# Moving steps of a hand-written order: the second layer's attention of a two-layer transformer on one core

## The chip, the core and the metric

The kernel runs on one core of a Trainium2 chip. The metric is the device time of one execution in microseconds (us). Before the change it is 630.8 us, the median of three runs (625.72 to 632.23). The core has five engines that each work through their own instructions in order: PE (TensorE, matrix products), DVE (VectorE), ACT (ScalarE), POOL (GpSimd) and SP (SyncE, here only a queue of DMA issues). An instruction that waits holds up everything behind it on its engine.

## What is computed

Two layers over x, 8 batches of 256 tokens with 128 channels. Each layer norms and modulates x by a per-batch condition, adds a gated causal attention with 16 heads, norms and modulates again, and adds a gated mixture of experts. Cut to the second layer, which the change is about (`ca`, `sa`, `ga`, `cb`, `sb`, `gb` are rows per batch):

```
h = layernorm(x) * (1 + ca) + sa
q, k, v = h @ w_q, h @ w_k, h @ w_v                  # 16 heads of 64
w = softmax(causal(q k^T) / 8)
x = x + ga * (concat(w v) @ w_o)
h = layernorm(x) * (1 + cb) + sb
r = sigmoid(h @ gate_w + gate_b); top 2 of 16 experts, values divided by their sum
x = x + gb * (h + shared_mlp(h) + sum of 2 expert mlps, weighted)
```

The second layer's attention needs x with the first layer's experts already added; the sparse experts of layer 2 need the choices of batches 0 to 5 (batches 6 and 7 go through all experts densely).

## The kernel before

In the profile layer 0 (its attention, then its experts) ends at about 263 us, layer 1's attention runs from 265.5 to 531 us, and layer 1's experts from 531 us to the end. Everything from layer 0's attention on is in an order written out by hand: the order of the Python calls is the order of each engine's instructions. The framework adds the waits and the buffers; a tile tag with n buffers makes the (n+1)th user wait for the first one's last reader. Tag `p` in PSUM has two buffers and serves every projection, norm transpose, choice and output product.

The attention works in 32 units, four per batch; unit n is batch n // 4, and covers four heads. For a unit `project_qk1` (L1548) makes q and k (eight 128x256 matmul records on PE at L1554, copied out by ACT at L1558), `scores1` (L1575) makes scores of four heads (PE L1585), exponentials (ACT L1588) and the causal mask (POOL `affine_select`, L812). Two units make a pair p = 0 to 15. `values1` (L1596) multiplies a pair's weights by v (PE L1613), copies the unnormalised output `ou` out (DVE L1617), and sums the weights (PE L1623). After the second pair of a batch `reciprocals1` (L1628) takes 1 / sum on DVE (L1630) and spreads it through DRAM to a tile `rb` by DMA (L1635, L1638). `normalise1` (L1645) multiplies `ou` by `rb`, four 128x512 DVE operations per batch (L1647). `finish1` (L1661) makes the output product `y` (PE L1667, 32 records) and adds it to x (DVE L1673, L1674).

The loop over pairs, with tables of steps (`first`, `mid`, `last`, `late`) that are run at fixed places of each pair; `heads` holds steps to run after one head's mask inside `scores1`:

```
for p in range(N // 2):
    scores(2 * p + 1)
    run(first, p)
    project(2 * p + 3)
    if p + 1 < N // 2: project_v1(p + 1, 0)
    run(mid, p)
    project(2 * p + 4)
    if p + 1 < N // 2: project_v1(p + 1, 1)
    run(last, p)
    scores(2 * p + 2)
    values1(p)
    if p % 2 and p + 1 < N // 2: reciprocals1(p // 2)
    run(late, p)
```

The steps in these tables, before the change:

- The first layer's experts' outputs: `gather(b, j)` (two indirect DMAs each, issued by POOL at L1047), `combine` (six DVE operations, L1365 to L1369). Batches 2 and 3 are gathered inside units 0 and 1, combined late in pair 0.
- The first norm: `measure` (DVE statistics L746, L748, then two small POOL operations L751, L752 for the reciprocal deviation), `normalise` (DVE L762), `modulate` (PE transposes L771, then h on DVE L774). Batch 1's measure and normalise stand ahead of pair 0, its modulate at `mid` 0, ahead of unit 4's projection.
- `sel`, a constant made by POOL (L2025, L2026) after unit 0's scores and needed only after the attention.
- `normalise1(b)` at `late` of pair 2b + 2, `finish1(b)` at `first` of pair 2b + 3.
- The second norm and the choice (`norm1`, `route1`, steps called `go`): batches 0 and 1 together from pair 5, 2 and 3 from pair 9, 4 from pair 11, 5 from pair 13. `route1` makes logits (PE L1716), the top two (17 short DVE operations, L1722 to L903), counts of earlier tokens (POOL `seen` L907, PE `rk` L910 and L911), slots (DVE `at` L913 to `idx` L919), then scatters of the tokens to DRAM by indirect DMA (POOL L924), one after a head's mask. `tokens` and `add` are POOL operations (L1690 to L1696).
- The tables of the experts' tiles (`tables_steps`, PE `cnt` L954, then 14 DVE operations L957 to L995) at `last` 14; they give the indices `widx` and `rowi` by which SP fetches experts' weights (L1771, `fetch_weights1`) and rows (L1749, `fetch_rows1`).

After pair 15 the experts begin with the transpose of the first fetched rows (PE L1786 `xT`).

Of the kernel before, what the change touches and what calls it, by code (L numbers as in the profile page):

```python
# [13 lines left out]
ALU = mybir.AluOpType  # L14
# [10 lines left out]
D0, D1 = 8, 64  # L25
# [532 lines left out]
def fast_path(ctx: ExitStack, tc: tile.TileContext, i: dict, out: bass.AP, bad: bass.AP):  # L558
# [300 lines left out]
    class Sorted:  # L859
# [184 lines left out]
        def gather(self, yg, j):  # L1044

            for k in range(2):
                nc.gpsimd.indirect_dma_start(  # L1047
                    out=yg[:, k, :], out_offset=None, in_=self.ys[:, :],
                    in_offset=bass.IndirectOffsetOnAxis(ap=self.yidx[:, j, k : k + 1], axis=0),
                )  # L1050
# [594 lines left out]
    def normalise1(b, u):  # L1645
        aT = st1["ou", b]
        nc.vector.tensor_tensor(aT[:, :, u, :], aT[:, :, u, :], st1["rb", b][:, :, u, :], ALU.mult)  # L1647
# [97 lines left out]
    def fetch_rows1(m):  # L1745

        xg = sq["x", m] = lp.tile([P, 4, P], F32, tag="xg", bufs=4, name=f"xg1_{m}")
        if m < E1 // 4:
            nc.sync.dma_start(  # L1749
                out=xg, in_=z1.xs.rearrange("(e r) c -> r e c", r=z1.cap)[0:P, bass.ts(m, 4), :]  # L1750
            )
        else:
            for t in range(4):
                z1.load_rows(xg[:, t, :], 4 * m + t - E1, starts.pop(0))

    def find_rows1(m):

        starts.extend(z1.row_starts(4 * m - E1, 4))
# [189 lines left out]
    def to(where, p, *steps):  # L1948
        where.setdefault(p, []).extend(steps)

    def at_scores(n, head, step):

        heads.setdefault(n, {}).setdefault(head, []).append(step)
# [5 lines left out]
    def combine_later(b):  # L1959
        return lambda: combine(b)  # L1960
# [6 lines left out]
    project_qk1(0, 1)  # L1967
    measure, normalise, modulate = layernorm_parts(0, md[1], SA, CA, "1a1", ps_ln, tiles=range(2, TT))
    for j in range(2):
        at_scores(0, 1 + 2 * j, lambda j=j: gather(2, j))  # L1970
        at_scores(1, 1 + 2 * j, lambda j=j: gather(3, j))
    to(first, -1, combine_later(1), measure, normalise)
    to(mid, 0, modulate)
    for w, n in ((1, 0), (2, 3), (3, 7)):
        measure, normalise, modulate = first_norm(w)
        if w == 1:
            to(late, 0, combine_later(2), combine_later(3), measure)
            to(late, 1, normalise)
        else:
            for k in range(4):  # L1980
                at_scores(8 * w - 13 + k, 3, lambda w=w, k=k: gather(2 * w + k // 2, k % 2))
            to(late, n, combine_later(2 * w))
            to(first, n + 1, combine_later(2 * w + 1))
            to(last, n + 1, measure)
            to(late, n + 1, normalise)
        to(mid, 4 * w - 2 if w == 1 else n + 2, modulate)
    for b in range(B - 1):
        to(late, 2 * b + 2, *[lambda b=b, u=u: normalise1(b, u) for u in range(4)])
        to(first, 2 * b + 3, lambda b=b: finish1(b))
    for bs in ((0, 2), (2, 2), (4, 1), (5, 1)):  # L1990
        p = 2 * sum(bs) + 1
        measure, normalise, modulate, tokens, add = norm1(bs)
        go = one(route1(bs))
        if bs[0] < 5:
            to(last, p, measure)
            to(late, p, normalise)
            to(first if bs[0] == 4 else mid, p + 1, modulate, tokens)
            to(last, p + 1, go)
            to(late, p + 1, go, go, go, go)
            to(mid, p + 2, go)  # L2000
            for k in range(4 * bs[1] - 1):
                at_scores(2 * p + 6 + k // 2, 1 + 2 * (k % 2), go)
            to(late, p + 3, add)
        else:
            to(first, p, measure)
            to(last, p, normalise, modulate, tokens)
            to(first, p + 1, go, go, go, go, go)
            to(last, p + 1, go)
            for k in range(3):
                at_scores(2 * p + 4, 1 + k, go)  # L2010
    tables = one(z1.tables_steps(ps_ln, True))
    to(last, 14, tables, lambda: fetch_weights1(4), lambda: fetch_weights1(5))
    to(first, 15, *[lambda m=m: fetch_rows1(m) for m in range(4)], *[lambda m=m: find_rows1(m) for m in range(4, NQ)],
       lambda: fetch_weights1(6))

    def scores(n):
# [3 lines left out]
    def project(n):  # L2020
        if n < N:
            project_qk1(*divmod(n, 4))

    scores(0)
    nc.gpsimd.memset(sel, 0.0)  # L2025
    nc.gpsimd.affine_select(  # L2026
        out=sel, in_=sel, compare_op=ALU.not_equal, fill=1.0, base=0,
        pattern=[[-8, 4], [-32, 2], [-64, 2], [0, D1]], channel_multiplier=1,
    )
    run(first, -1)  # L2030
    project(2)
    for p in range(N // 2):
# [3 lines that stand above are left out]
        if p + 1 < N // 2:  # L2036
            project_v1(p + 1, 0)
        run(mid, p)
        project(2 * p + 4)
        if p + 1 < N // 2:  # L2040
            project_v1(p + 1, 1)
        run(last, p)
        scores(2 * p + 2)
        values1(p)
        if p % 2 and p + 1 < N // 2:
            reciprocals1(p // 2)
        run(late, p)
# [209 lines left out]
```

## Time and profile before

| what | us |
|---|---|
| median of three runs (lowest, highest) | 630.8 (625.72, 632.23) |
| the profiled execution, its own time | 630.67 |
| its span, first to last instruction | 628.6 |
| PE busy, DVE, POOL, ACT | 541.1, 326.6, 309.9, 265.6 |
| mean granted TensorE clock | 0.94 |
| PE busy in 265 to 290, 290 to 525, 525 to 575, 575 to 630 | 18.66, 223.42, 43.85, 32.19 |

The profile is of one execution. Busy time is the time in which an engine has an instruction in work; matmuls overlap, so PE can be busy for the whole of a stretch. A view by windows gives the busy time of each engine in stretches; here the stretches are the pairs, each from the start of `scores(2p+1)` to that of the next. A view of waits gives who waited for whom. The timeline gives instructions in order, in columns start, duration, engine, line, operation, output and inputs, count, and in brackets the idle time ahead of it and what ended it. The chain of waits goes back from the last instruction through what released each step.

### The profile page before, as it was taken

Reading aid. Unit: us, or ns where it says so; the run is one execution under the profiler, and the core shown is the slowest. Engines: PE = TensorE matmul, PEld = TensorE weight load, DVE = VectorE, ACT = ScalarE, POOL = GpSimd, SP = SyncE. Lnnn points to the kernel's source line nnn. Section 1 sums busy time; section 2 is a strip of 40 time slices with the busy share of each in tenths; the row PEclk is TensorE's granted clock in tenths of the full one; section 3 lists DMA queues with packets and bytes.
Section 4 is the critical chain, followed back from the end, with each engine's and each line's share of the span. In section 5 each row is a group of like instructions: output and inputs, shape, how many; then the busy total and the mean of one; then the engine's idle time right before and its main releaser. Section 6 shows DMA issues by size and latency. Waiting matters only on the chain.

```text
span 628.6 us, 11934 instructions
## 1 busy us (share of the span) xinstructions
PE 541.1 (86%) x4391; PEld 389.3 (62%) x4391; DVE 326.6 (52%) x1031; ACT 265.6 (42%) x489; POOL 309.9 (49%) x472
## 2 busy tenths in 40 slices
PE   3799879878799999687999999989998898888961
PEld 3344435445699998455777767667776666665451
DVE  3347896856732222311543645473544676654683
ACT  1475675546065555162544353433534432330330
POOL 7356686866314441365551444572356664203760
PEclk9998988879999999896999999999999999888996
DMA  8999980120329996040030303030203036562431
GB/s 279 346 407 404 388 315 13 61 90 29 113 82 328 327 321 214 22 163 22 19 86 2 72 15 86 15 85 5 69 9 90 10 90 177 164 183 73 113 90 56
DMA packets 52909, 85.38 MB, mean 136 GB/s; under 512 B 6428, under 2 KB 32156, under 8 KB 51692
## 3 DMA queue, kind: packets, MB, share of 16 engines
q1 hardware_dynamic: 44444, 59.77, 29.9%
q0 software_dynamic: 8400, 24.78, 12.7%
q8 instruction: 36, 0.59, 0.4%
q14 instruction: 29, 0.24, 0.1%
HBM read 53.46 MB, written 31.07 MB: 134 GB/s over the span
## 4 chain that ended last, share of the span: by engine, by line
PE 58%; DVE 18%; POOL 8%; DMA 6%; issue 4%; ACT 4%; SPq 0%; DVEq 0%; POOLq 0%; ACTq 0%
PE o L1613 7%; PE hp L1338 6%; PE sc L1585 5%; PE yt L1346 5%; POOL yg L1047 5%; PE qp L1554 4%; PE kp L1554 4%; PE vp L1567 4%; PE sc L1137 3%; DVE ou L1647 3%; PE y L1667 3%; PE sum L1623 3%; PE o L1162 2%; PE qk L1101 2%; PE gu L1797 1%
## 5 line engine op out<-in xcount | busy, mean ns | idle before, releaser
L812 POOL TENSOR_SCALAR_AFFINE_SELECT pt<-pt 128x256 f32<-128x256 f32 (+1 forms) x176 | 91.1, 542 | 90.4 <-ACT pt L1588 59.9
L1588 ACT ACTIVATE pt<-sc 128x768 f32<-128x768 f32 x64 | 48.5, 808 | 71.1 <-PE sc L1585 70.9
L1047 POOL DMA_INDIRECT yg<-ys,yidx x56 | 54.3, 969 | 29.7 <-issue 14.6
L1617 DVE COPY ou<-o 128x512 f32<-128x512 f32 x32 | 22.0, 691 | 68.9 <-PE o L1613 68.9
L1141 ACT ACTIVATE pt<-sc 128x1024 f32<-128x1024 f32 x48 | 46.5, 1022 | 17.6 <-PE sc L1137 14.4
L1039 POOL DMA_INDIRECT wt<-in_wpk_dram,widx x31 | 29.1, 939 | 48.8 <-PE xT L1329 47.3
L1340 ACT ACTIVATE hst<-hp,wt 128x128 f32<-128x128 f32 x136 | 38.8, 367 | 30.0 <-ACT hst L1340 17.9
L1585 PEld LDWEIGHTS sc<-q,k 64*128 64x128 f32 x512 | 41.8, 188 | 15.5 <-issue 12.4
L1585 PE MATMUL sc<-q,k 64*128 64x256 f32 (+1 forms) x512 | 50.8, 338 | 0.0
L1558 ACT COPY q<-qp 128x512 f32<-128x512 f32 x32 | 18.7, 585 | 63.1 <-PE qp L1554 62.6
L1613 PE MATMUL o<-pt,v 128*64 128x256 f32 (+1 forms) x512 | 45.1, 329 | 0.0
L1137 PE MATMUL sc<-qm,k 32*128 32x512 f32 x192 | 38.3, 731 | 3.9 <-ACT pt L1141 3.0
L1350 DVE COPY ysb<-yt 128x128 f32<-128x128 f32 x39 | 11.4, 292 | 58.0 <-PE yt L1346 58.0
L1554 PE MATMUL qp<-h,wq 128*128 128x256 f32 x128 | 36.8, 412 | 4.7 <-DVE h L774 1.5
L1613 PEld LDWEIGHTS o<-pt,v 128*64 128x64 f32 x512 | 32.0, 137 | 11.2
L1667 PE MATMUL y<-wo,ou 128*128 128x128 f32 x256 | 34.2, 291 | 5.1 <-DVE ou L1647 5.0
L1338 PE MATMUL hp<-xTs,wt 128*128 128x128 f32 x272 | 36.9, 279 | 1.6 <-DMA wt<-in_wpk_dram,widx 0.9
L924 POOL DMA_INDIRECT xs<-ht0b,idx x32 | 31.6, 988 | 13.5 <-issue 4.7
L1554 PE MATMUL kp<-h,wk 128*128 128x256 f32 x128 | 35.6, 403 | 0.7 <-DVE t L1673 0.5
L1667 PEld LDWEIGHTS y<-wo,ou 128*128 128x128 f32 x256 | 31.5, 200 | 7.3 <-DVE ou L1647 6.2
L1346 PE MATMUL yt<-wt,hst 128*128 128x128 f32 x272 | 35.8, 275 | 0.0
L1567 PE MATMUL vp<-wv,h 128*128 128x512 f32 x64 | 35.6, 643 | 0.0
(292 smaller groups left out, 1095.2 us busy)
## 6 DMA issues: line engine op xcount, KB each, us to landing
xs<-zero SPq DMA_DIRECT2D x1, 12288.0 KB, 57.5
xs<-zero SPq DMA_DIRECT2D x1, 8192.0 KB, 26.4
rb<-rd SPq DMA_DIRECT2D x14, 512.0 KB, 5.8
mdb<-mrd SPq DMA_DIRECT2D x2, 2048.0 KB, 7.3
xg<-xs SPq DMA_DIRECT2D x63, 64.0 KB, 4.1
wt<-in_wpk_dram SPq DMA_DIRECT2D x24, 128.0 KB, 2.3
wst<-in_wpk_dram SPq DMA_DIRECT2D x5, 514.0 KB, 12.7
ys<-ysb SPq DMA_DIRECT2D x10, 256.0 KB, 2.7
```

The costliest lines, as they stand in the source:

```text
L812: nc.gpsimd.affine_select(out=pt, in_=pt, compare_op=ALU.is_ge, fill=0.0, base=0, pattern=[[0, pt.shape[1]], [1, P]], channel_multiplier=-1,)
L1047: nc.gpsimd.indirect_dma_start(out=yg[:, k, :], out_offset=None, in_=self.ys[:, :], in_offset=bass.IndirectOffsetOnAxis(ap=self.yidx[:, j, ...
L1137: nc.tensor.matmul(out=sc[:, n, :].rearrange("p (a q) -> p a q", q=rhs.shape[2]), lhsT=k[r, cols], rhs=rhs, start=True, stop=True,)
L1141: nc.scalar.activation(pt[:, bass.ts(half, 2), :], sc, AF.Exp)
L1338: nc.tensor.matmul(out=hp[:, c, :], lhsT=wt[:, bass.ts(c, P)], rhs=xT, start=True, stop=True)
L1346: nc.tensor.matmul(out=y, lhsT=hs[:, c, :], rhs=wt[:, bass.ds(WF + c * P, P)], start=(c == 0), stop=(c == FC - 1))
L1554: nc.tensor.matmul(out=ps_[:, n, :], lhsT=w1[f"w{what}1"][:, bass.ts(2 * u + n, P)], rhs=hb, start=True, stop=True)
L1567: nc.tensor.matmul(out=vp, lhsT=hb[:, bass.ts(j, P)], rhs=w1["wv1"][:, bass.ts(half, 512)], start=True, stop=True)
L1585: nc.tensor.matmul(out=sc[:, n, cols], lhsT=k[r, m, bass.ts(kb, P)], rhs=q[r, m, qs], start=True, stop=True)
L1588: nc.scalar.activation(pt, sc[:, :, 0:384], AF.Exp, scale=1.0 / math.sqrt(D1))
L1613: nc.tensor.matmul(out=os_[u][bass.ts(n, D1), m, qs], lhsT=v[:, kb, bass.ts(4 * k + 2 * m + n, D1)], rhs=pts[u][m][:, n, cols], start=(kb ...
L1667: nc.tensor.matmul(out=y[:, j, :], lhsT=aT[:, c % 2, c // 2, bass.ts(j, P)], rhs=w1["wo1"][:, c, :], start=(c == 0), stop=(c == NC1 - 1),)
```

## The change

Only the places of steps in the tables change; every engine executes as many instructions as before, in another order.

- The gathers of batches 2 and 3 move one unit later, to units 1 and 2. Batch 1's normalise moves to `mid` 0, its modulate to `first` 1, and unit 4's projection behind it. `combine` of batch 3 and the measure of batches 2 and 3 move into pair 1. `sel` is made at `mid` 3.
- `normalise1(b)` moves from `late` 2b + 2 to `mid` 2b + 3 (for b = 5 to `first` 13), `finish1(b)` from `first` to `last` of the same pair (for b = 5 to `mid` 13).
- Batch 4's modulate moves from `first` 12 to `mid` 12. Batch 5's measure, modulate and choice move later: measure to `mid` 13, modulate to `first` 14, directly ahead of its logits.
- The tables move from `last` 14 to `first` 15, the fetches of rows from `first` 15 to `mid` 15, after batch 6's normalise1.

```diff
@@ -1967,26 +1967,24 @@
     project_qk1(0, 1)
     measure, normalise, modulate = layernorm_parts(0, md[1], SA, CA, "1a1", ps_ln, tiles=range(2, TT))
     for j in range(2):
-        at_scores(0, 1 + 2 * j, lambda j=j: gather(2, j))
-        at_scores(1, 1 + 2 * j, lambda j=j: gather(3, j))
-    to(first, -1, combine_later(1), measure, normalise)
-    to(mid, 0, modulate)
+        at_scores(1, 1 + 2 * j, lambda j=j: gather(2, j))
+        at_scores(2, 1 + 2 * j, lambda j=j: gather(3, j))
+    to(first, -1, combine_later(1), measure)
+    to(mid, 0, normalise)
+    to(first, 1, modulate, lambda: project(4))
     for w, n in ((1, 0), (2, 3), (3, 7)):
         measure, normalise, modulate = first_norm(w)
-        if w == 1:
-            to(late, 0, combine_later(2), combine_later(3), measure)
-            to(late, 1, normalise)
-        else:
+        if w > 1:
             for k in range(4):
                 at_scores(8 * w - 13 + k, 3, lambda w=w, k=k: gather(2 * w + k // 2, k % 2))
-            to(late, n, combine_later(2 * w))
-            to(first, n + 1, combine_later(2 * w + 1))
-            to(last, n + 1, measure)
-            to(late, n + 1, normalise)
-        to(mid, 4 * w - 2 if w == 1 else n + 2, modulate)
+        to(late, n, combine_later(2 * w))
+        to(first, n + 1, combine_later(2 * w + 1))
+        to(last, n + 1, measure)
+        to(late, n + 1, normalise)
+        to(mid, n + 2, modulate)
     for b in range(B - 1):
-        to(late, 2 * b + 2, *[lambda b=b, u=u: normalise1(b, u) for u in range(4)])
-        to(first, 2 * b + 3, lambda b=b: finish1(b))
+        to(first if b == 5 else mid, 2 * b + 3, *[lambda b=b, u=u: normalise1(b, u) for u in range(4)])
+        to(mid if b == 5 else last, 2 * b + 3, lambda b=b: finish1(b))
     for bs in ((0, 2), (2, 2), (4, 1), (5, 1)):
         p = 2 * sum(bs) + 1
         measure, normalise, modulate, tokens, add = norm1(bs)
@@ -1994,7 +1992,7 @@
         if bs[0] < 5:
             to(last, p, measure)
             to(late, p, normalise)
-            to(first if bs[0] == 4 else mid, p + 1, modulate, tokens)
+            to(mid, p + 1, modulate, tokens)
             to(last, p + 1, go)
             to(late, p + 1, go, go, go, go)
             to(mid, p + 2, go)
@@ -2002,15 +2000,15 @@
                 at_scores(2 * p + 6 + k // 2, 1 + 2 * (k % 2), go)
             to(late, p + 3, add)
         else:
-            to(first, p, measure)
-            to(last, p, normalise, modulate, tokens)
-            to(first, p + 1, go, go, go, go, go)
+            to(mid, p, measure)
+            to(last, p, normalise)
+            to(first, p + 1, modulate, tokens, go, go, go, go, go)
             to(last, p + 1, go)
             for k in range(3):
                 at_scores(2 * p + 4, 1 + k, go)
     tables = one(z1.tables_steps(ps_ln, True))
-    to(last, 14, tables, lambda: fetch_weights1(4), lambda: fetch_weights1(5))
-    to(first, 15, *[lambda m=m: fetch_rows1(m) for m in range(4)], *[lambda m=m: find_rows1(m) for m in range(4, NQ)],
+    to(first, 15, tables, lambda: fetch_weights1(4), lambda: fetch_weights1(5))
+    to(mid, 15, *[lambda m=m: fetch_rows1(m) for m in range(4)], *[lambda m=m: find_rows1(m) for m in range(4, NQ)],
        lambda: fetch_weights1(6))
 
     def scores(n):
@@ -2021,12 +2019,15 @@
         if n < N:
             project_qk1(*divmod(n, 4))
 
+    def make_sel():
+        nc.gpsimd.memset(sel, 0.0)
+        nc.gpsimd.affine_select(
+            out=sel, in_=sel, compare_op=ALU.not_equal, fill=1.0, base=0,
+            pattern=[[-8, 4], [-32, 2], [-64, 2], [0, D1]], channel_multiplier=1,
+        )
+
+    to(mid, 3, make_sel)
     scores(0)
-    nc.gpsimd.memset(sel, 0.0)
-    nc.gpsimd.affine_select(
-        out=sel, in_=sel, compare_op=ALU.not_equal, fill=1.0, base=0,
-        pattern=[[-8, 4], [-32, 2], [-64, 2], [0, D1]], channel_multiplier=1,
-    )
     run(first, -1)
     project(2)
     for p in range(N // 2):
@@ -2036,7 +2037,8 @@
         if p + 1 < N // 2:
             project_v1(p + 1, 0)
         run(mid, p)
-        project(2 * p + 4)
+        if p:
+            project(2 * p + 4)
         if p + 1 < N // 2:
             project_v1(p + 1, 1)
         run(last, p)
```

## The prediction, made before the changed kernel ran

> **What bounds the kernel now.** I read the page first (which engines the chain of waits runs through), then the windows with one row per pair of layer 1's attention, then PE's waits in that stage, then the timeline where a pair is long.
>
> ```profile
> PE 58%; DVE 18%; POOL 8%; DMA 6%; issue 4%; ACT 4%; SPq 0%; DVEq 0%; POOLq 0%; ACTq 0%
> ```
> ```profile
> core 0: us, PE busy (x) PEld busy (x) DVE busy (x) ACT busy (x) POOL busy (x), PEclk, DMA share, GB/s
> 276.42:298.87 22.45, 16.64 (x120) 11.02 (x119) 3.49 (x10) 7.50 (x13) 14.72 (x23) 0.77 0.09 24
> 342.34:355.12 12.78, 12.78 (x118) 8.87 (x118) 10.06 (x29) 6.54 (x10) 4.70 (x10) 1.00 0.37 85
> 386.94:404.31 17.37, 16.94 (x156) 12.81 (x152) 8.57 (x28) 6.54 (x10) 7.16 (x16) 1.00 0.04 12
> 417.03:439.03 22.00, 19.56 (x158) 14.86 (x154) 10.08 (x20) 6.54 (x10) 10.31 (x15) 0.92 0.03 9
> 470.84:486.16 15.32, 13.60 (x126) 9.53 (x122) 6.03 (x11) 6.77 (x11) 8.99 (x15) 1.00 0.37 88
> 486.16:505.46 19.30, 17.54 (x156) 13.17 (x153) 12.07 (x35) 6.64 (x10) 13.06 (x21) 1.00 0.05 15
> 505.46:519.05 13.59, 12.14 (x119) 8.18 (x115) 11.38 (x37) 5.49 (x9) 7.64 (x14) 1.00 0.44 99
> 519.05:531.08 12.03, 10.12 (x117) 8.06 (x113) 7.88 (x13) 1.51 (x2) 6.89 (x11) 1.00 0.66 188
> ```
> These are pairs 0, 4, 7, 9, 12, 13, 14 and 15. Pair 4 has nothing added and PE is busy for all of its 12.78 us: PE is the bound, and only PE's waits can be won or lost. Pair 0 loses most, then pair 9.
>
> ```profile
> PE nt1a L771 <- DVE xn1a L762: 5.1, 1, 5.1
> PE y L1667 <- DVE ou L1647: 5.0, 5, 1.1
> PE nt1b L771 <- DVE xn1b L762: 1.7, 1, 1.7
> PE rk L910 <- DVE m L903: 1.2, 1, 1.2
> ```
> The 5.1 is in pair 0. Its cause stands on POOL: two gathers, `sel`, and only then the deviation that batch 1's normalise needs:
>
> ```profile
> 282.18 0.97 POOL L2025 MEMSET sel<- 128x1024 f32 x1
> 283.22 1.20 POOL L2026 TENSOR_SCALAR_AFFINE_SELECT sel<-sel 128x1024 f32<-128x1024 f32 x1
> ...
> 285.99 0.75 PE L771 MATMUL nt1a<-ident,xn1a 128*128 128x128 f32 x2 [5.08 <-DVE xn1a L762]
> ...
> 287.47 2.05 PE L1554 MATMUL qp<-h,wq 128*128 128x256 f32 x4 [0.73 <-DVE h L774]
> ```
> The reader sees the wait, and behind it a projection at 2.05 that takes 1.06 warm: the granted clock fell.
>
> **Part by part.** I walk PE through each changed pair, T being the start of its `scores(2p+1)`. Sizes from rows: scores 1.51, q and k of a unit 1.9, v 0.95, values 2.75, sums 1.44, y 3.78.
>
> *Pairs 0 and 1.* POOL now does the deviation right behind unit 0's masks, so normalise is done near 279. Pair 0 loses unit 4's q and k and has no wait: after v(1,0) at 280.9 come v 0.95, scores 1.51, values and sums 4.19, so pair 1 begins at 287.6, not 298.87. Unit 0 and 1's masks are ready: the last is behind two gather issues (1.26 each) at 282.7, values begin at 283.4. Pair 1 takes its 12.84 plus 1.9 plus transposes 0.4 plus a wait for h of 0.95 (DVE is free of the combine of batch 2 at 289.1; the row of before has 0.73): 16.1. It ends at 303.7 against 311.71: **-8.0**. Ends: -8.9 (no wait), -5.5 (the combine, queued ahead of h on DVE, waits for a gather that lands 3 us later). The combine of batch 3 is behind h and holds nothing that PE needs. `sel`, 2.2 on POOL at pair 3, lies in POOL's idle time: POOL is busy 2.96 of 16.37 there; with that gone it would cost its 2.2.
>
> *Pairs 3 and 5.* y moves behind the projections. The multiplications (4 for 2.49 at 355.36) are still done in time: DVE reaches them before y's turn. Projections directly behind scores are paced by ACT's copies (5.59 in pair 4, 5.4 behind y in pair 3): **+0.5** for both; ends 0 and +0.6.
>
> *Pairs 7 and 11.* Here I see a loss. Before, DVE had nothing else to do when `at` came. Now DVE does the choice first (17 operations, 388.64 to 392.87, 4.2; now from T-0.6 to T+3.65), then the four multiplications (2.49, to T+6.15), and only then `at`. `rk` is at T+5.1 behind POOL's `seen` (1.38), and the second projection needs `rk`'s PSUM buffer, which `at` frees: the waits have "qp <- DVE at" already, 0.3 each. So PE, through with v at T+4.4, goes on at T+6.45, and all its work is queued behind; then 2.92 for q, k, v (395.63 to 398.55) and 3.78 for y: the next scores at T+13.15, against 11.61 before. With 0.15 for `seen` beside the multiplications: +1.7 each, **+3.4**. Ends: +0.3 each if the wait is only that for `seen` (0.6 less the 0.3 of before), +2.9 each if all of `seen` delays DVE.
>
> *Pair 9.* y waited in pieces for multiplications that took 5.29 instead of 2.49, beside POOL's `add` (1.28 and 1.61), and the clock fell (0.92). Now DVE does them behind h, at T+6.2 to T+8.7, when `add` is through (T+4.5); y's turn comes at T+8.3, four records per 0.47. No wait: the next scores at T+12.0 against T+16.3: **-4.3**. Ends: -3.4 (0.96 of delay beside POOL, the least of the three contended rows) and -4.8 (all that pair 9 has over 17.2, which is 12.78, 3.78 and transposes 0.6).
>
> *Pair 12.* The transposes go behind q, k and v, when `xn` is ready: the 1.7 wait goes, ACT's pacing takes 0.2: **-1.5**; ends -1.7 and -1.0.
>
> *Pair 13.* The multiplications took 4.93 beside `add` of batches 2 and 3, y waited 0.97, k 0.49, q 0.31. Now choice (3.6 long) from T-0.7, multiplications T+3.1 to about T+5.9, y T+4.4 to T+8.3, then `t` and `x` (0.85) ahead of `at`, so q goes on at T+9.6; next scores T+12.5 against 13.6: **-1.1**; ends -1.8 and 0.
>
> *Pair 14.* Modulate now stands directly ahead of the logits. Transposes end at T+1.9, but DVE is in 1/sum (1.76) and its two judgements until T+2.85, then h 0.54: logits at T+3.45, a PE wait of 1.55. The choice starts 1.3 later than before; `rk`, which waited 1.2 for it already, comes 1.3 later; 0.3 of `cnt` moves out: **+1.0**; ends 0 and +2.0.
>
> *Pair 15.* The largest loss. The tables' 14 operations were on DVE from 514.14 to 519.85, beside PE's values of pair 14:
>
> ```profile
> 519.39 0.46 DVE L995 TENSOR_SCALAR widx<-expert_t,wnum_t 128x24 int32<-128x24 f32 x1
> 519.76 1.28 DVE L1617 COPY ou<-o 128x512 f32<-128x512 f32 x2
> 520.96 3.45 DVE L1647 TENSOR_TENSOR ou<-ou,rb 128x512 f32<-128x512 f32 x4
> ...
> 524.46 2.50 PE L1667 MATMUL y<-wo,ou 128*128 128x128 f32 x20 [0.86 <-DVE ou L1647]
> ```
> They delayed the copies and cost y waits of 1.06 and 0.86 only. Now they start behind `cnt`, at T+1.85, and run 5.44 to T+7.3; the multiplications come behind them, and nothing is left for PE but y: it starts at T+8.0, after 6.2 idle. The last multiplication ends between T+9.8 (2.49) and T+10.6 (with the 0.96 more of the row above, beside POOL); half of y's last quarter and the second half follow, 2.36, then values and sums 4.19: T+16.75. The clock: the 5.1 wait of pair 0 made the next three groups cost 2.05, 1.91, 1.91 for 1.06, 0.86, 0.99, 2.96 lost. Part of that hides under DVE's pace; I take 1.2. T+17.95 against 12.03: **+5.9**. Ends: +4.3 (T+9.8, no clock loss), +8.1 (2.96, T+10.6, 0.4 more for rows). Behind the tables SP is late too: eight weight issues 4.68, then rows, landing 5.0 at the median: the first at about T+17.6, so the first `xT` is near both limits. The experts' stage, 97.5 us from `xT` on, moves as a whole.
>
> Two rules speak to this. The Trainium skill's TensorE: Matmul & The Clock Gate, section "Part 1: The HAM clock gate", says that PE falls to half clock after an idle window of about 3.4 us and needs about as long a busy one to return: it speaks against the new wait in pair 15, and the row of pair 0 agrees. By the rule alone the loss would be half of 3.4, an estimate of 1.7, so pair 15 would be +6.4 and the sum -3.6. Its SBUF — State Buffer, section "SBUF: two separate sides", says that a VectorE operation with two SBUF inputs and a GpSimd operation that reads SBUF lock each other out entirely. The 5.29 and 4.93 agree, 2.80 and 2.44 beyond 2.49 for 2.89 of POOL; the masks at 356.98 beside multiplications took 2.21 for 1.48 and DVE none more. By the rule alone `seen` would cost all its 1.38 in pairs 7 and 11, and the sum would be -1.6.
>
> **Sum:** -8.0 +0.5 +3.4 -4.3 -1.5 -1.1 +1.0 +5.9 = -4.1. Against the profiled execution's own 630.67 (span 628.6 and 2.1 around it), which is 0.1 under the median of the runs, 630.8: **626.6 us**. All best ends give -12.3, all worst +6.6.
>
> **Rivals.**
> A, the late stalls are small: the second projection of pairs 7 and 11 waits only for `seen` (+0.6 for both, not +3.4) and pair 15 keeps its clock (+4.3): 630.67 - 8.5 = 622.2. For: neither wait is in the trace of before at this size. Against: DVE's queue order is in the code.
> B, the clock stays low: half clock after pair 0's wait lasted from 286 to 293; if y and the values of pair 15 all lose as that did, pair 15 costs +8.1: 628.8. For: 6.2 idle is longer than 5.1.
> C, slower: SP becomes the bound behind the late tables. Its place is pair 15: weights (4.68), rows (2.05), six index loads (2.6 between rows and the next weights), weights (3.03) and rows (6.12) are one queue that starts at T+7.9. If the experts' PE work then runs behind SP by two fetches of four tiles, 3.03 and 4.68, the sum turns to +3.6: 634.3; it decides from 4.1 on. For: the chain has SP and a weight landing of 3.38 at 555 to 560. Against: PE is as late as SP.
>
> **How the numbers follow.** Forecast 0.52, A 0.20, B 0.16, C 0.12. Range 621.5 to 633.5: left out are the third of A that lies lowest (0.06), the half and more of C that lies highest (0.07), and runs as far from the median as the lowest before, 5 us (0.07): 2 in 10. The forecast's own range is 624 to 630. One per cent, 6.3 us, is about what a measurement of this kernel can tell from no change. Faster by over that (under 624.4): 0.18 of A and 0.04 of the forecast, 0.22. Slower (over 637.1): 0.08 of C. Within: 0.70.
>
> **What would show it.** Right: no wait at `nt1a` in pair 0, pairs 0 and 1 together 27.2; pair 9 near 17.7 at clock 1.00; pair 7 and 11 near 19.0, with PE waiting for `at`; a wait of 1.5 for logits in pair 14; in pair 15 y waiting some 6 for `ou`, and half clock behind it. Wrong: pair 15 under 15 (A), or waits of the experts for weights that were not there before (C).

## The result, and the profile after

The changed kernel takes 627.72 us (median of 20 runs, 624.91 to 631.37) against 630.64 for the kernel before (20 runs, 625.68 to 632.81): a ratio of 0.9966, with a 95% interval of 0.9943 to 0.9989. That is 2.9 us, well inside the one per cent that was called no change, and 1.1 above the forecast of 626.6. The profiled execution of the changed kernel took 625.22 (span 623.2), below its own median, so the pairs are compared, not the spans.

The chain of waits (first line of the profile page's part on it) has given PE a per cent more, and VectorE three:

```profile
PE 59%; DVE 21%; POOL 6%; issue 4%; ACT 3%; DMA 3%; SPq 1%; DVEq 0%; POOLq 0%; ACTq 0%
```

The windows of the changed kernel, for the same pairs as before (0, 4, 7, 9, 12, 13, 14 and 15; columns: stretch, its length, busy time of each engine with its instructions, granted clock, DMA share, GB/s):

```profile
core 0: us, PE busy (x) PEld busy (x) DVE busy (x) ACT busy (x) POOL busy (x), PEclk, DMA share, GB/s
275.51:286.50 10.99, 10.99 (x110) 7.53 (x109) 3.65 (x12) 6.34 (x11) 9.47 (x17) 1.00 0.10 25
...
332.91:345.70 12.79, 12.79 (x120) 8.89 (x116) 9.98 (x28) 6.54 (x10) 4.71 (x10) 1.00 0.36 85
...
377.64:395.99 18.35, 16.85 (x155) 12.81 (x151) 8.88 (x28) 6.53 (x10) 8.23 (x16) 1.00 0.04 12
...
408.78:426.14 17.36, 17.12 (x157) 12.99 (x153) 7.78 (x20) 6.53 (x10) 9.94 (x15) 1.00 0.04 12
...
459.07:473.16 14.09, 13.63 (x126) 9.72 (x123) 5.96 (x12) 6.76 (x11) 9.82 (x15) 1.00 0.38 96
473.16:492.62 19.46, 17.47 (x154) 12.96 (x150) 11.62 (x33) 6.53 (x10) 12.45 (x19) 1.00 0.05 15
492.62:507.75 15.13, 13.62 (x121) 9.68 (x117) 9.59 (x29) 5.59 (x9) 8.82 (x16) 0.89 0.38 89
507.75:526.68 18.93, 11.36 (x117) 9.69 (x114) 11.08 (x21) 1.51 (x2) 6.48 (x11) 0.82 0.42 118
```

Pair 0 is all PE now, pair 9 almost so. Pairs 7, 14 and 15 have become longer, pair 15 by more than half, and PE is idle for four tenths of it (7.6 of 18.9). PE's waits in layer 1's attention, from pair 0 to the first `xT` (called the stage from here on), name what did it (columns: total, times, longest):

```profile
PE y L1667 <- DVE ou L1647: 9.0, 2, 7.6
PE rk L911 <- POOL seen L907: 2.0, 2, 1.0
PE lg L1716 <- DVE h L774: 1.5, 1, 1.5
...
PE qp L1554 <- DVE at L913: 1.0, 2, 0.5
```

The waits for `xn1a` (5.1) and `xn1b` (1.7) are gone. New are one of 7.6 in pair 15, one of 1.4 in pair 13 (both in the first line), the two of 1.0 for `seen` in pairs 7 and 11, and the 1.5 in pair 14.

By pair, in us, from the windows of each profile. "Before again" is a second execution of the kernel before, which was profiled among the experiments. (The prediction's rows for pairs 7 and 9 end some 0.07 late, at 17.37 and 22.00; here they are 17.30 and 21.93.)

| pairs | before | before again | after | forecast | measured, against the first |
|---|---|---|---|---|---|
| 0 and 1 | 35.29 | 33.87 | 26.72 | -8.0 | -8.57 |
| 3 and 5 | 33.66 | 33.67 | 33.80 | +0.5 | +0.14 |
| 7 and 11 | 34.60 | 34.61 | 36.70 | +3.4 | +2.10 |
| 9 | 21.93 | 21.35 | 17.36 | -4.3 | -4.57 |
| 12 | 15.32 | 15.33 | 14.09 | -1.5 | -1.23 |
| 13 | 19.30 | 19.31 | 19.46 | -1.1 | +0.16 |
| 14 | 13.59 | 15.21 | 15.13 | +1.0 | +1.54 |
| 15 | 12.03 | 10.40 | 18.93 | +5.9 | +6.90 |
| all 16 | 254.66 | 252.70 | 251.17 | -4.1 | -3.49 |

The five pairs not listed changed by 0.05 or less each. Behind the first `xT` the experts' stage takes 96.5 for 97.6 (94.8 in the second execution of before). So the large terms were real and nearly cancel: 14.4 us won in pairs 0, 1, 9 and 12, 10.9 lost elsewhere.

### The profile page after: what moved, and what is told of

The parts are those of the page before. It is cut to its first block, busy times and chain, and to the rows that moved or that the text cites. A ratio compares the mean times of both kernels' runs of the same rounds, so it can differ in the third digit from the quotient of the medians.

```text
span 623.2 us, 11938 instructions
## 1 busy us (share of the span) xinstructions
PE 535.6 (86%) x4391; PEld 387.9 (62%) x4391; DVE 327.7 (53%) x1031; ACT 266.0 (43%) x489; POOL 311.7 (50%) x472
## 4 chain that ended last, share of the span: by engine, by line
PE 59%; DVE 21%; POOL 6%; issue 4%; ACT 3%; DMA 3%; SPq 1%; DVEq 0%; POOLq 0%; ACTq 0%
PE o L1613 7%; PE sc L1585 7%; PE hp L1338 6%; PE yt L1346 6%; PE qp L1554 5%; PE y L1667 5%; POOL yg L1047 4%; PE vp L1567 4%; PE kp L1554 4%; PE sum L1623 3%; PE sc L1137 2%; PE qk L1101 1%; DVE ou L1647 1%; PE hp L1272 1%; PE ysh L1291 1%
## 5 line engine op out<-in xcount | busy, mean ns | idle before, releaser
L1137 PE MATMUL sc<-qm,k 32*128 32x512 f32 x192 | 36.6, 698 | 4.5 <-ACT pt L1141 3.7
L1667 PE MATMUL y<-wo,ou 128*128 128x128 f32 x256 | 32.6, 288 | 9.1 <-DVE ou L1647 9.0
L1338 PEld LDWEIGHTS hp<-xTs,wt 128*128 128x128 f32 x272 | 33.0, 192 | 3.6 <-issue 1.7
```

Source lines behind the costliest of these rows:

```text
L1137: nc.tensor.matmul(out=sc[:, n, :].rearrange("p (a q) -> p a q", q=rhs.shape[2]), lhsT=k[r, cols], rhs=rhs, start=True, stop=True,)
L1338: nc.tensor.matmul(out=hp[:, c, :], lhsT=wt[:, bass.ts(c, P)], rhs=xT, start=True, stop=True)
L1667: nc.tensor.matmul(out=y[:, j, :], lhsT=aT[:, c % 2, c // 2, bass.ts(j, P)], rhs=w1["wo1"][:, c, :], start=(c == 0), stop=(c == NC1 - 1),)
```

## The experiments

Theory: each pair has its own account, settled by the wait that ends last in it, and the accounts add. Rivals: gains are given back where later work comes due; or a pair is long for where y stands and not for what VectorE does ahead of it. The first four ran on a chip on which every kernel takes some 25 us more, nearly all of it behind the first `xT` (119.4 to 120.0 for 94.8 to 98.0: ACT waits 26.0 to 27.4 there, once, for something that the profile does not name). Their ratios are to the kernel before on that chip, 656.72; the changed kernel was not run there, so with it only pairs are compared. Where there was a single run, its whole time is not used.

### Tables back in pair 14

```diff
-    to(first, 15, tables, lambda: fetch_weights1(4), lambda: fetch_weights1(5))
-    to(mid, 15, *[lambda m=m: fetch_rows1(m) for m in range(4)], *[lambda m=m: find_rows1(m) for m in range(4, NQ)],
+    to(last, 14, tables, lambda: fetch_weights1(4), lambda: fetch_weights1(5))
+    to(first, 15, *[lambda m=m: fetch_rows1(m) for m in range(4)], *[lambda m=m: find_rows1(m) for m in range(4, NQ)],
```

> The changed kernel with one step undone: the tables and the fetches of weights 4 and 5 stand again at the end of pair 14, the fetch of rows at the head of pair 15. Theory (each pair has its own account, and pair 15's loss of 6.9 us is that of the tables ahead of the multiplications on VectorE): pair 15 is back to 12.0 to 12.5 us, pairs 0 to 14 stay within 0.2 of the changed kernel's, the half clock of 513.9 to 520.7 is gone, and the time is 6.5 below the changed kernel's: about 621. Rival (pair 15 is long because the multiplications and y stand behind the projections, whatever DVE does ahead of them): pair 15 stays above 16 and the time is within 2 of the changed kernel's.

Measured: pair 15 12.05, the stage 246.73 for 251.17, 645.85 us for 656.72 of before, ratio 0.9827 (0.9789 to 0.9864). Pair 15 of this run (windows as above):

```profile
512.72:524.77 12.05, 10.11 (x117) 8.07 (x113) 7.89 (x13) 1.51 (x2) 6.89 (x11) 1.00 0.64 188
```

Pairs 0, 2 to 5 and 7 to 14 are within 0.2 of the changed kernel's; pairs 1 and 6 are 0.9 and 1.2 longer on that chip. The theory holds: the tables' place is worth 6.9 us, over twice the 2.9 that the whole change gained.

### Only the first pairs' step

```diff
-        at_scores(0, 1 + 2 * j, lambda j=j: gather(2, j))
-        at_scores(1, 1 + 2 * j, lambda j=j: gather(3, j))
-    to(first, -1, combine_later(1), measure, normalise)
-    to(mid, 0, modulate)
+        at_scores(1, 1 + 2 * j, lambda j=j: gather(2, j))
+        at_scores(2, 1 + 2 * j, lambda j=j: gather(3, j))
+    to(first, -1, combine_later(1), measure)
+    to(mid, 0, normalise)
+    to(first, 1, modulate, lambda: project(4))
```
(with batch 2's norm in the loop and `sel` at pair 3, all as in the change)

> The kernel before with only the step of pairs 0 and 1: the gathers one unit later, batch 1's normalise and modulate in pairs 0 and 1, projection of unit 4 behind it, choice table at pair 3, batch 2 in the loop. Everything of the output products, of the later norms and of the tables is as before. Theory: pairs 0 and 1 take 26.7 together for 35.3, all later pairs are as before to 0.2, and the whole 8.6 reaches the end: about 622. Rival (part of it is given back where later work comes due, in the pairs that wait for SP's or POOL's work or in the experts' stage): the time falls by less than 5, and some later pair or the stage behind the first xT is longer than before by the difference.

Measured: 646.05 for 656.72, ratio 0.9815 (0.9765 to 0.9864), 10.7 less where 8.6 was expected. Pairs 0 and 1 take 28.22 here, where 26.7 was expected; on the same chip, the kernel of the run with only the products moved, which has the old code there, takes 33.93. So the pairs show 5.7 of the 10.7; the profiled execution was the slowest of the four (652.42), and where the rest lies is not shown. Of the later pairs two were not as before to 0.2: pair 14 took 14.17 for 13.59, and pair 12 17.39 for 15.32, since its wait for `xn1b` was 2.2 for 1.7 this time and half clock followed (a projection at 1.90 for 1.03). The time falls by more than 5 all the same, so the rival falls.

### Batch 6's products ahead of the late tables

```diff
-        to(first if b == 5 else mid, 2 * b + 3, *[lambda b=b, u=u: normalise1(b, u) for u in range(4)])
+        to(first if b == 5 else late if b == 6 else mid, 2 * b + (2 if b == 6 else 3), *[lambda b=b, u=u: normalise1(b, u) for u in range(4)])
```

> The changed kernel with only the multiplications of batch 6 moved ahead of the tables on VectorE; the tables, the fetches of weights and rows stay in pair 15. Theory A (the 7.6 us that y waits is the whole cost of the late tables): y no longer waits, pair 15 is 12 to 12.5 long, and the time is 6.5 below the changed kernel's, 621. Theory B (SyncE's order is the bound right behind it: the tables end at 516.3, eight weight issues take 4.7, then rows are issued that land some 5 us later): the first xT can't come before about 17.6 us into pair 15, PE waits for a DMA instead of VectorE, and the time falls by 1 to 2 only, to 626.

Measured: pair 15 18.12 for 18.93; 654.47 for 656.72, ratio 0.9896 (0.9816 to 0.9977). Theory B holds. The timeline of this run, PE, VectorE's last table and SP's issues:

```profile
515.75 3.82 PE L1667 MATMUL y<-wo,ou 128*128 128x128 f32 x32
...
522.37 0.72 DVE L995 TENSOR_SCALAR widx<-expert_t,wnum_t 128x24 int32<-128x24 f32 x1
...
523.65 4.67 SPq L1771 DMA_DIRECT2D wt<-in_wpk_dram  x8
528.42 2.05 SPq L1749 DMA_DIRECT2D xg<-xs  x4
532.32 1.09 PE L1786 MATMUL xT<-ident,xg 128*128 128x128 f32 x4 [8.41 <-DMA xg<-xs]
```

y runs without a wait, and PE then idles 8.4 for the rows: they are issued behind the tables and eight weight issues. In the changed kernel two bounds of about one height stand behind the late tables; taking one away gives 0.8 in pair 15, and 0.4 in pairs 14 and 15 together (33.64 for 34.06).

### Only the products of batches 0 to 4 and 6 moved

```diff
-        to(late, 2 * b + 2, *[lambda b=b, u=u: normalise1(b, u) for u in range(4)])
-        to(first, 2 * b + 3, lambda b=b: finish1(b))
+        to(late if b == 5 else mid, 2 * b + (2 if b == 5 else 3), *[lambda b=b, u=u: normalise1(b, u) for u in range(4)])
+        to(first if b == 5 else last, 2 * b + 3, lambda b=b: finish1(b))
```

> The kernel before with only the multiplications by 1/sum and the output products of batches 0 to 4 moved behind the projections of the pair (batch 5 as before, and batch 6 as in the kernel before); the first norm, the choices, the tables are as before. Theory: pair 9 loses its 4.6 (22.0 to 17.4) and pairs 7 and 11 pay 1.0 each, as VectorE reaches the multiplications behind the choice and POOL's count is slowed beside them; the sum is -2.6: 628. Rival (the 1.0 of pairs 7 and 11 comes from elsewhere in the change): pairs 7 and 11 are as before to 0.2, the sum is -4.6: 626.

Measured: pair 9 17.35, pairs 7 and 11 18.36 each; 654.82 for 656.72, ratio 0.9980 (0.9945 to 1.0014), an interval that includes no change. The pairs are as the theory has it, and the 1.0 of pairs 7 and 11 is this step's. The edit moves batch 6's products too, as the change does, though the expectation says otherwise. With the tables still in pair 14 that costs nothing: pair 15 takes 12.03, as before.

### The ranks ahead of the products in pairs 7 and 11

The new lines stand behind the loop that enters `go`; this run and the next two have the tables back in pair 14 as well.

```diff
-        to(first if b == 5 else mid, 2 * b + 3, *[lambda b=b, u=u: normalise1(b, u) for u in range(4)])
+        if b not in (2, 4):
+            to(first if b == 5 else mid, 2 * b + 3, *[lambda b=b, u=u: normalise1(b, u) for u in range(4)])
...
+    for b in (2, 4):
+        to(mid, 2 * b + 3, *[lambda b=b, u=u: normalise1(b, u) for u in range(4)])
```

> The changed kernel with the tables back in pair 14, and in pairs 7 and 11 the step that ranks (rk, at) ahead of the four multiplications on VectorE instead of behind them. Theory (the 1.0 of each pair is rk's wait for a count on POOL that is slowed beside the multiplications, and the next projection's wait for at behind them): both pairs are back to 17.3 from 18.35, and no wait of y comes in their place, as VectorE reaches the multiplications by about 6 us into the pair and y's turn is at 8. Rival (the multiplications behind at are too late for y): the waits for the count go, y waits for ou by about as much, and the pairs stay at 18 or more.

Measured: 17.15 each, a little better than the kernel before (17.30). The timeline of pair 7 in the changed kernel:

```profile
381.06 2.55 DVE L1647 TENSOR_TENSOR ou<-ou,rb 128x512 f32<-128x512 f32 x4
...
381.23 2.45 POOL L907 TENSOR_TENSOR seen<-seen,m 128x16 bf16<-128x16 bf16 x4 [3.50 <-DVE m L903]
...
383.12 0.19 PE L911 MATMUL rk<-seen,allb 128*128 128x64 bf16 x1 [1.01 <-POOL seen L907]
...
383.80 1.13 PE L1554 MATMUL qp<-h,wq 128*128 128x256 f32 x4 [0.49 <-DVE at L913]
```

The same pair in this run:

```profile
380.84 1.10 POOL L907 TENSOR_TENSOR seen<-seen,m 128x16 bf16<-128x16 bf16 x4 [3.50 <-DVE m L903]
...
381.70 0.19 PE L911 MATMUL rk<-seen,allb 128*128 128x64 bf16 x1
...
382.21 1.13 PE L1554 MATMUL qp<-h,wq 128*128 128x256 f32 x4 [0.32 <-DVE at L913]
...
383.04 2.69 DVE L1647 TENSOR_TENSOR ou<-ou,rb 128x512 f32<-128x512 f32 x4
...
385.03 3.74 PE L1667 MATMUL y<-wo,ou 128*128 128x128 f32 x32
```

Beside the multiplications POOL's four small operations took 2.45 for 1.10, while the multiplications lost next to nothing. With the order turned, the count is done before they start, and y still does not wait.

### POOL's additions for batches 2 and 3 earlier

```diff
-            to(late, p + 3, add)
+            if bs[0] == 2:
+                to(last, p + 3, add)
+            else:
+                to(late, p + 3, add)
```

> The changed kernel with the tables back in pair 14, and POOL's two additions for batches 2 and 3 (1.28 each) issued at the end of pair 12's projections instead of behind its masks at the end of the pair, so that they no longer run beside the choice of pair 13. Theory (the two small operations of the choice that took 1.30 for 0.19 were locked out by POOL's additions): the choice takes 3.6 again for 5.8, y waits 0 for ou instead of 1.4, and pair 13 takes 17.5 to 18.0 for 19.47; pair 12 stays within 0.3. Rival (the small operations are slow for another reason, or POOL's masks come late behind the additions): pair 13 stays above 19, or pair 12 grows by over 1.

Measured: pair 13 17.22 for 19.46, pair 12 14.08; pairs 14 and 15 together 27.47, with the tables' step alone 27.26. The timeline of pair 13 in the changed kernel:

```profile
473.27 1.33 DVE L841 TENSOR_TENSOR teq<-p,g 128x32 f32<-128x32 f32 x1
473.27 1.27 POOL L1695 TENSOR_TENSOR xn1b<-ht,mdb 128x512 f32<-128x512 f32 x1
...
474.62 1.27 POOL L1696 TENSOR_TENSOR x<-x,xn1b 128x512 f32<-128x512 f32 x1
474.63 1.30 DVE L842 TENSOR_TENSOR teq<-teq,rank 128x32 f32<-128x32 f32 x1
...
479.04 4.46 PE L1667 MATMUL y<-wo,ou 128*128 128x128 f32 x32 [1.42 <-DVE ou L1647]
```

The same pair in this run:

```profile
473.41 0.19 DVE L841 TENSOR_TENSOR teq<-p,g 128x32 f32<-128x32 f32 x1
473.64 0.19 DVE L842 TENSOR_TENSOR teq<-teq,rank 128x32 f32<-128x32 f32 x1
...
477.60 3.79 PE L1667 MATMUL y<-wo,ou 128*128 128x128 f32 x32
```

An operation of 0.19 started at the same instant as POOL's 1.27 and came out 1.33 later; the next met the second addition. The two took 2.63 for 0.38, the multiplications started 2.25 later, and y paid 1.4 in waiting and 0.7 in its own length.

### Batch 5's modulate ahead of the division

```diff
-            to(first, p + 1, modulate, tokens, go, go, go, go, go)
+            for step in (modulate, tokens):
+                at_scores(2 * p + 2, 3, step)
+            to(first, p + 1, go, go, go, go, go)
```

> The changed kernel with the tables back in pair 14, and batch 5's modulate and tokens at the last scores of pair 13 instead of at the head of pair 14, so that h is written before the division and the judgements on VectorE. Theory (pair 14's extra is the wait of 1.5 to 2.0 for h, and a half clock of 3.4 us behind it): no wait for h, no half clock, pair 14 takes 13.0 to 13.6 for 15.1 to 15.5, and pair 13 grows by 0.4 at most for the transposes. Rival (the clock falls there for the light work of the logits, not for the wait): the wait goes, the half clock stays, and pair 14 takes 14 or more.

Measured: the wait for `h` is gone, and pair 14 takes 15.24 all the same: PE waits 1.3 for the choice's `m` at `rk` instead, and the clock is half for 3.4. But pair 15 takes 10.42 for 12.05. The two windows of this run:

```profile
496.09:511.33 15.24, 13.76 (x119) 9.31 (x115) 12.99 (x41) 5.59 (x9) 9.56 (x16) 0.89 0.40 92
511.33:521.75 10.42, 9.73 (x116) 7.92 (x112) 6.31 (x9) 1.51 (x2) 6.14 (x9) 1.00 0.73 211
```

Both pairs together take 25.66 for 27.26, which is the kernel before's 25.62; pair 13 pays 0.37 for it (19.85 for 19.48). What the rival forecast for pair 14 came in, but its clock is not what the pair costs. The two pairs have one bound: VectorE's chain of division, choice, tables, multiplications. The last table, `widx`, ends 14.4 us into pair 14 here, and 14.4 in both executions of before, of which one has the half clock in pair 14 and one has not; with the tables alone back it ends at 16.0. What PE does in pair 14, at whichever clock, lies beside this chain. The choice starts 2.8 us into the pair here, for 4.1 in the changed kernel, and what that wins shows one pair later, at y.

### All four together

> The changed kernel with all four steps: the tables back in pair 14, the ranks first in pairs 7 and 11, POOL's additions earlier, batch 5's modulate earlier. Theory (the pairs' accounts add): 6.9 + 2.1 + 1.7 + 1.8 = 12.5 less than the changed kernel in layer 1's attention, 238.7 for 251.2, or 16 less than the kernel before (ratio about 0.975). Rival (waits move from pair to pair): the stage takes more than 242.

Measured: the stage takes 238.47, 12.7 less than in the changed kernel; 613.81 us (6 runs, 612.37 to 617.56) against 629.08 for before on the same chip, ratio 0.9753 (0.9719 to 0.9788). The accounts add, if pairs 14 and 15 are one account: 6.8 for the tables, 2.4 for the ranks, 2.25 for the additions, and 1.2 for batch 5's modulate (1.6 less pair 13's 0.37) make 12.7. This version beats the kernel before by 2.5%, and the changed kernel by the stage.

### POOL's order of the first pairs alone, and the norm's place alone

On the kernel before, the gathers and `sel`, which goes from behind `scores(0)` to `mid` 3:

```diff
-        at_scores(0, 1 + 2 * j, lambda j=j: gather(2, j))
-        at_scores(1, 1 + 2 * j, lambda j=j: gather(3, j))
+        at_scores(1, 1 + 2 * j, lambda j=j: gather(2, j))
+        at_scores(2, 1 + 2 * j, lambda j=j: gather(3, j))
...
-    nc.gpsimd.memset(sel, 0.0)
...
+    to(mid, 3, make_sel)
```

> The kernel before with only POOL's order of pairs 0 and 1 changed: the gathers for batches 2 and 3 one unit later, and the choice table at pair 3. Batch 1's normalise and modulate stay where they were, and unit 4's q and k stay in pair 0. Theory (the wait of 5.1 for xn1a and the half clock behind it, 2.96, come from four gathers and the table ahead of the deviation on POOL, and not from where modulate stands): no wait at nt1a, no half clock, pair 0 takes 14.2 to 14.8 for 22.45, pairs 0 and 1 together 27 to 27.7 for 35.3; all of the step's gain without moving the norm. Rival (the norm must be moved as well, as DVE's combine ahead of it is late by itself): pairs 0 and 1 together stay above 30.

The other run is the changed kernel with these two edits taken back.

> The changed kernel with POOL's order of pairs 0 and 1 as before: the gathers for batches 2 and 3 at the scores of units 0 and 1, the choice table behind the scores of unit 0; normalise, modulate and unit 4's projection at their new places. Theory: the transposes no longer wait, but the masks of unit 1 come behind gathers, table and deviation, some 4 to 5 us after values need them, so that PE waits for POOL in pair 0 instead: pairs 0 and 1 together 30 to 33 for 26.7. Rival (POOL's order matters little once modulate stands a pair later): 27.5 or less.

Measured: pairs 0 and 1 together 26.87 with POOL's order alone (14.03 and 12.84, a little under what was expected), 32.68 with the norm's place alone, 26.72 with both. The timeline of the first run:

```profile
278.02 0.72 POOL L752 TENSOR_TENSOR rstd1a<-rstd1a,minus_half 128x2 f32<-128x2 f32 x1
...
281.17 0.38 PE L771 MATMUL nt1a<-ident,xn1a 128*128 128x128 f32 x2
...
282.28 1.10 PE L1554 MATMUL qp<-h,wq 128*128 128x256 f32 x4 [0.73 <-DVE h L774]
```

The deviation is done 2.4 ahead of the transposes, and the clock stays whole. In the second run the transposes stand a pair later, and PE waits for masks that stand behind gathers, table and deviation:

```profile
286.88 1.23 PE L1613 MATMUL o<-pt,v 128*64 128x256 f32 x8 [1.23 <-POOL pt L812]
...
290.12 1.32 PE L1613 MATMUL o<-pt,v 128*64 128x256 f32 x8 [2.01 <-POOL pt L812]
```

So all but 0.15 of the largest gain is POOL's order. Moving batch 1's norm and unit 4's projection was not needed.

### The additions earlier in the kernel before

```diff
-            to(late, p + 3, add)
+            if bs[1] == 2:
+                to(last, p + 3, add)
+            else:
+                to(late, p + 3, add)
```

> The kernel before with only POOL's additions (L1695, L1696) for batches 0 and 1 moved from behind pair 8 to the end of its projections, and those for batches 2 and 3 likewise in pair 12; the multiplications and y stay where they are. Theory (VectorE's multiplications and POOL's additions lock each other out in SBUF): the four multiplications of pair 9 take 2.5 for 5.29 and those of pair 13 2.5 for 4.93, y's waits in pieces go, so does the half clock of pair 9; pair 9 takes 17.3 to 18.5 for 21.93 and pair 13 17.4 to 18.3 for 19.30; pairs 8 and 12 grow by 0.3 at most. Rival (y in pieces is slow because it stands too close behind the multiplications): the multiplications stay over 4, or pair 9 stays above 20.5.

Measured: pair 9 18.63 for 21.35 and 21.93 in the two executions of before, at clock 1.00 for 0.92; pair 13 17.19 for 19.30; pairs 8 and 12 12.79 and 15.34, as before. Pair 9 ends 0.13 above the range that was expected and pair 13 0.21 below its own. VectorE's multiplications and POOL's additions in pair 9 of the kernel before, first execution:

```profile
417.54 5.29 DVE L1647 TENSOR_TENSOR ou<-ou,rb 128x512 f32<-128x512 f32 x4
...
418.51 1.28 POOL L1695 TENSOR_TENSOR xn1b<-ht,mdb 128x512 f32<-128x512 f32 x1
...
419.86 1.61 POOL L1696 TENSOR_TENSOR x<-x,xn1b 128x512 f32<-128x512 f32 x1
```

The multiplications and the product in this run:

```profile
420.35 3.10 DVE L1647 TENSOR_TENSOR ou<-ou,rb 128x512 f32<-128x512 f32 x4
...
421.08 4.92 PE L1667 MATMUL y<-wo,ou 128*128 128x128 f32 x32 [0.18 <-DVE ou L1647]
```

3.10 for 5.29 (2.5 was expected; masks still run beside them), and in pair 13 2.49 for 4.93. So about 3 (2.7 to 3.3) of pair 9's 4.0 to 4.6 is the collision with POOL and what follows from it, and 1.27 (18.63 less 17.36) the products' place. With the additions out of the way, the old place is the better one in pair 13 (17.19 against 19.46) and spares pairs 7 and 11 their 1.0.

### The kernel before once more

> The kernel before, unchanged, as the measure for the pairs of the three others: if a pair's time is a property of the program, all 16 are within 0.2 of the first profile but for pairs 0 to 2, which wait for gathers. If the half clock falls by chance, pairs 0, 9 or 12 differ by 1 to 2.

Twelve pairs agree within 0.02 with the first profile, four differ: pairs 0 and 9, of those that the expectation named, by 1.43 and 0.58, and 14 and 15, which it did not name, by 1.6 each. Pairs 0, 9, 14 and 15 of this second execution (windows as above):

```profile
274.77:295.79 21.02, 15.21 (x119) 10.48 (x119) 3.36 (x9) 7.50 (x13) 14.72 (x23) 0.84 0.10 26
...
413.98:435.33 21.35, 19.01 (x156) 14.48 (x152) 10.07 (x20) 6.53 (x10) 10.30 (x15) 0.92 0.03 9
...
501.86:517.07 15.21, 13.77 (x119) 9.17 (x115) 12.96 (x41) 5.59 (x9) 8.37 (x15) 0.89 0.37 93
517.07:527.47 10.40, 9.73 (x116) 7.92 (x113) 6.29 (x9) 1.51 (x2) 6.15 (x9) 1.00 0.75 213
```

Twice the missing clock times the length is the time at half clock: in pair 0 6.7 us here, 10.3 in the first profile (0.77 of 22.45), in pair 14 3.3 here and none there. Pair 9 has 0.92 in both, but the half clock stands at another place: 6.2 us into the pair in the first profile, where PE is busy for all of the 3.41, and 4.6 here, where PE is busy for 3.02 of them and waits for the rest. That this makes the 0.58 is likely and not shown. Pairs 14 and 15 trade 1.62 for 1.63, as a common bound must; pair 0's 1.4 stays. Against this execution the change gains 1.5 us in the stage, against the first 3.5.

## Why the prediction was right, point by point

*Pairs 0 and 1* (-8.0, measured -8.6, and -7.2 against the second execution). Right in size and in cause: POOL, not the norm's place; the prediction did not separate them, the last runs did. `sel` at pair 3 costs nothing: pair 3 takes 16.37 with it in the run with POOL's order alone and 16.36 before, and 16.44 in the changed kernel, with it, as in the run with the norm's place alone, without it.

*Pairs 3 and 5* (+0.5, measured +0.14). The loss was taken from the difference of two rows and is smaller than that; that ACT's copies are its cause was not shown.

*Pairs 7 and 11* (+3.4, measured +2.1). The queue was read rightly: `rk` for `seen`, then the projection for `at`. Only sizes were off: PE went on at T+6.16 for 6.45 (the multiplications ran from T+3.4 to T+6.0), q, k, v and y then took 6.49 for 6.70, and the 0.15 for `seen` did not come on top: 0.65 less in each pair. It was POOL that was slowed, by 1.35 a pair, within the time that PE lost anyway to `at`. Rival A's +0.6 is wrong as well.

*Pair 9* (-4.3, measured -4.6). Right, and the reason that was given first, multiplications beside POOL's additions, is the larger part, about 3.

*Pair 12* (-1.5, measured -1.2). Right.

*Pair 13* (-1.1, measured +0.16). This step failed. It has "choice (3.6 long) from T-0.7, multiplications T+3.1 to about T+5.9, y T+4.4 to T+8.3". The choice took 5.8, from T-0.7 to T+5.1, and y waited 1.4. The prediction had moved the multiplications away from the additions and did not ask what would stand there in their place: the choice, which is in front of them on the same engine. The row for it was in hand, that of pair 7, but with no POOL work beside it. The Trainium skill's SBUF — State Buffer, section "SBUF: two separate sides", says of a VectorE operation with two SBUF inputs and a GpSimd operation that reads SBUF that whichever starts first gets the shared ports for its whole instruction, and the other fully blocks; the 1.33 for 0.19 beside a 1.27 agrees. The prediction applied that rule to the multiplications and to `seen`, and not to the choice's short operations.

*Pairs 14 and 15* (+6.9 together, measured +8.4 against either execution of before). The prediction kept two accounts, with pair 14's as a wait of PE; they are one account, and VectorE's. Of the 8.4, the tables' place is 6.5 to 6.8 (34.06 less 27.26 to 27.54, the three runs with the tables back and batch 5's modulate still late) and batch 5's late modulate 1.6 to 1.9 (those less 25.66). For the first, the timeline of the changed kernel:

```profile
509.26 0.18 PE L954 MATMUL cnt<-seen,allb 128*128 128x16 bf16 x1
...
511.24 0.74 POOL L1695 TENSOR_TENSOR xn1b<-ht,mdb 128x256 f32<-128x256 f32 x1
511.28 1.13 DVE L978 TENSOR_TENSOR on_t<-nums,first_t 128x384 f32<-128x384 f32 x1
...
515.55 0.71 DVE L995 TENSOR_SCALAR widx<-expert_t,wnum_t 128x24 int32<-128x24 f32 x1
516.18 2.48 DVE L1647 TENSOR_TENSOR ou<-ou,rb 128x512 f32<-128x512 f32 x4
...
517.01 5.56 PE L1667 MATMUL y<-wo,ou 128*128 128x128 f32 x32 [7.57 <-DVE ou L1647]
```

The tables took 6.8 for 5.44 (`cnt` to `widx`'s end 7.0): five of them were slower by 0.1 to 0.6, beside POOL's additions for batches 4 and 5 or its masks, most of all `on_t`, 1.13 for 0.55. That was not in the sum. The multiplications took 2.48, and y 5.56 for 3.78 at half clock, a loss of 1.8 where 1.2 was taken. (The prediction's upper end for pair 15, +8.1, leaves out its own 0.4 for rows; with it, it would be +8.5.) The estimate of 1.7 for this place, half of the 3.4 that the Trainium skill's TensorE: Matmul & The Clock Gate, section "Part 1: The HAM clock gate", gives as the window, was nearer. That is partly luck: the clock was half for about 6.8 in this pair (0.82 of 18.93), of which y met about half.

*Rival C* did not come in: PE is not behind SP, and the first `xT` does not wait. But its bound lay just beneath, as the run with batch 6's products first shows (pair 15 at 18.12 for 18.93).

*The sum.* The errors are -0.6, -0.4, -1.3, -0.3, +0.3, +1.3, +0.5 and +1.0, +0.6 in all with the unlisted pairs. A net figure as good as this is partly luck: the loss in pairs 7 and 11 was put too high by as much as pair 13 fell short.

What stays open: which instant lets the clock fall where waits are short, and what ACT waited for on the one chip. That POOL's order together with the earlier additions, both in the kernel before, would give 240.9 for the stage is worked out (245.90 less 2.93 and 2.11) and was not run.

## What to carry to other kernels

When two engines slow each other, look first for an operation that nobody waits for soon (here POOL's additions) and move that, before the one in the queue of the bound: in pair 13 what took the multiplications' place met the same neighbour. In pair 9 nothing did, and both moves helped. When a serial chain on one engine crosses several stages, account for the chain as a whole: in pairs 14 and 15 a wait taken out of one pair came back in the next, or was won there. And a change made of several moves is best judged move by move: here one move ate two thirds of the gain of the others.

## What was not expected of the hardware

- The granted clock is not a property of the program. Two executions of one program differ in where it is half, in lengths of about 3.4 us or a multiple (3.3, 6.7, 10.3 above), and all of the difference of their attention stages, 2.0 us, is in pairs in which it is half. The Trainium skill's TensorE: Matmul & The Clock Gate, section "Part 1: The HAM clock gate", says that the window is free-running and does not reset when a kernel starts; the two executions agree. Its table has the clock fall after an idle window of some 3.4 us. Here it fell in pair 14 of the second execution with no wait over 1.3, after 3.41 us in which PE was busy for 1.97; so short waits among light work were enough. In the run with the tables alone back a wait of 2.0 in the same pair left the clock whole.
- Half clock costs nothing where another engine is the bound: pair 14 with pair 15 takes 25.62 without it and 25.61 with it.
- Either engine can be the one that is slowed when VectorE and POOL meet: VectorE in pair 13 (1.33 for 0.19) and pair 9 (5.29 for 2.5), POOL in pair 7 (2.45 for 1.10, the multiplications 2.55).
